# A two-layer graph convolution on one core: the last chunk sums interleaved with block 47's products, and block 48 placed in turned form

## The chip, the core and the metric

The kernel runs on one core of a Trainium2 chip. The metric is device time in microseconds (us). The kernel before took 2044.03 us in the median of three runs (2043.89 to 2047.14).

## The reference, cut to what matters

`x` is 6250 nodes by 512 features in fp32; `src` and `dst` are the 100,000 edges, sorted by `dst`. Two Chebyshev convolutions of order two follow each other:

```
h   = relu(layernorm(x))
deg = number of edges that leave a node;  dinv = deg > 0 ? 1 / sqrt(deg) : 0
conv(h, W0, W1, b) = h @ W0 + prop(h) @ W1 + b
prop(h)[n] = sum over edges e with dst[e] == n of  -dinv[src[e]] * dinv[n] * h[src[e]]
y   = leaky_relu(layernorm(conv(h, W1_0, W1_1, b1)) * gamma + beta)
out = x + conv(y, W2_0, W2_1, b2)
```

## The kernel before, in words

**Tiling.** Nodes are cut into 49 blocks of 128 rows (block 48 has 106). Edges are cut into 782 chunks of 128. Three chunks make a unit, four units a group, so there are 66 groups; group 0 holds one unit, group 65 the chunks 771 to 781 (its fourth unit has two chunks). Because `dst` is sorted, a unit's 384 edges fall into a window of 32 nodes, and a group's four windows stand below each other in the 128 rows of a PSUM tile.

**One group, in both layers.** GpSimd (POOL) gathers each chunk's 128 source rows from a table in DRAM by an indirect DMA (L444) into a ring of 55 places. VectorE (DVE) makes `sel`, a 0/1 matrix from edges to the window's 32 nodes (`choose`, L571); in layer 0 it scales `sel` by a column of the gathered rows (`scale`, L610). TensorE (PE) multiplies `sel` with the gathered rows, one matmul of 32 output rows and 512 columns for each chunk, summing a unit's three chunks into that unit's 32 rows (`sums`, L621). ScalarE (ACT) copies the 128 rows to SBUF (`agg`, L631).

**One block.** `place` (L651) moves the rows of the two or three groups that overlap the block to their place by 0/1 matrices `there` (made in `spots`, L639). ACT copies the result out, times `-dinv` (`an`, L704). Four PE transposes (L711) and a DVE copy (`aT`, L713) turn it, and `products` (L532) multiplies with the weights: four matmuls over slices `kc` of 128 features. The own-row product `h @ W0` is added in the same PSUM tile, or, for blocks 46 to 48 (`EARLY`), was computed earlier and is kept in `pre`. `finish` ends the block. In layer 0 that is the layer norm on DVE with steps on ACT (L671 to L688), then two writes by SyncE's queue (SP): the scaled rows to layer 1's table `tab[1]` (L685) and the rows themselves to `h_tab` (L690). In layer 1 it is an add (L660 for the last three blocks) and the write of the output (L665).

**Between the layers.** Layer 1's first 24 chunks are gathered before the last three blocks' rows exist (`gather_ahead`, L454): indices of those blocks are held to a row of zeros, and what is missing is added later by matmuls (L627) with counts that DVE and PE make from the edge list (`count_late`, L588 and L592). All later gathers of layer 1 (L444) wait until the last rows are in `tab[1]`.

**Order.** PE, POOL and SP run in the order in which the program is written; DVE and ACT are ordered by a scheduler, held back where the program says `issue_after`. In group step 64 (`g == NS - 2`) the code places block 47, sums units 0 and 1 of group 65 (six matmuls), turns block 47, places group 64's part of block 48 (`between`), multiplies block 47, and in the step of group 65 sums its units 2 and 3 (five matmuls). Then `turn` and `dense` do block 48: place group 65's part, copy out, transpose, copy, four products, `finish`. Only groups 64 and 65 overlap block 48.

Of the kernel before, what the change touches and what calls it, by code (L numbers as in the profile page):

```python
# [2 lines left out]

# [404 lines left out]
def usual_path(tc, have):  # L408
# [18 lines left out]
    with ExitStack() as es:  # L427
# [5 lines left out]
        own_h, own_x, agg, placed, started, pre, late, theres = {}, {}, {}, {}, {}, {}, {}, {}  # L433
        SHIFTED = D - D % P
        lidx = pool.tile([P, NC - SHIFTED], I32, name="lidx", bufs=1)

        def zr(layer, t):
            return places[:, (layer * NC + t) % R, :D]
# [91 lines left out]
        def products(u_ps, hT, w, r, start, stop):  # L530
            for kc in range(KD):
                nc.tensor.matmul(u_ps[:r], hT[:, kc, :r], w[:, kc, :], start=(start and kc == 0),  # L532
                                 stop=(stop and kc == KD - 1))

# [64 lines left out]
        def scale(sel, chunk, of=(0, NQ)):  # L599

            at = chunk[0][0]
            start = chunk[of[0]][0]
            end = chunk[min(of[1], len(chunk)) - 1][-1] + 1
            if end <= RAW:
                return
            each = sel.rearrange("p q s e -> p (q s) e")
            cut = sorted({start, end} | {t for t in range(start, end) if t % R == 0})
            for lo, hi in zip(cut, cut[1:]):
                v = each[:, lo - at : hi - at, :]
                last = nc.vector.tensor_tensor(  # L610
                    v, v, places[:, lo % R : lo % R + hi - lo, D : D + 1].to_broadcast([P, hi - lo, Q]), op=OP.mult)
            return last

        def sums(layer, g, sel, chunk, cnt=None, of=(0, NQ)):

            n = len(chunk)
            if of[0] == 0:
                summed[0] = psum.tile([P, D], F32, name="ps")
            ps = summed[0]
            for s, q in [(s, q) for s in range(STEP) for q in range(*of) if q < n and s < len(chunk[q])]:  # L620
                nc.tensor.matmul(ps[q * Q : (q + 1) * Q, :], sel[:, q, s, :], zr(layer, chunk[q][s]), start=(s == 0),  # L621
                                 stop=(s == len(chunk[q]) - 1 and (cnt is None or chunk[q][0] >= AHEAD_OF)))
# [6 lines left out]
            if of[1] >= n:  # L629
                agg[g] = pool.tile([P, D], F32, name="agg", bufs=3)  # L630
                nc.scalar.activation(agg[g][: n * Q], ps[: n * Q], AF.Copy)  # L631

# [10 lines left out]
        def place(i, some):  # L643

            r = rows[i]
            if i not in placed:
                placed[i] = psum.tile([P, D], F32, name="an_ps", bufs=1)
            there = theres.pop(i) if i in theres else spots(i, some)
            for t, g in zip(there, some):
                m = Q * (unit[g + 1] - unit[g])  # L650
                nc.tensor.matmul(placed[i][:r], t[:m, :r], agg[g][:m, :], start=(g == inside[i][0]),  # L651
                                 stop=(g == inside[i][-1]))

        def finish(layer, i, v):
            r = rows[i]
# [65 lines left out]
        def second(layer, i, aT):  # L721
            w1 = w_late[:, 0] if layer else w_sb[0]
            whole = i not in started
            u_ps = psum.tile([P, D], F32, name="u_ps") if whole else started.pop(i)
            products(u_ps, aT, w1, rows[i], whole, True)
            finish(layer, i, u_ps)
# [74 lines left out]
        for layer in range(2):  # L801
            if layer == 1:
                gathered = AHEAD_OF
                for i in range(AHEAD):
                    load(layer, i)
            i, chosen, left = 0, {}, []
            for g in range(NS):
                gather_to(layer, STEP * unit[g] + R)
                if layer == 0 and g == NS // 2:
                    for k, w in enumerate((W2_1, W2_0)):  # L810
                        nc.sync.dma_start(w_late[:, k], w.rearrange("(k p) d -> p k d", p=P))
                if layer == 0:
# [20 lines left out]
                of = (NQ // 2, NQ) if g == NS - 1 else (0, NQ)  # L833
                if layer == 0 and g < NS - 1:
                    with ExitStack() as order:
                        for ins in behind.values():
                            order.enter_context(tc.issue_after(ins.ins))
                        scaled = scale(sel, chunk)
                if g < NS - 1:
                    chosen[g + 1] = choose(g + 1)  # L840
                sums(layer, g, sel, chunk, count_late(sel, chunk) if layer == 1 else None, of)
                if layer == 0 and g == 1:
                    widen()
                if layer == 0 and g == NS - 16:
                    with tc.issue_after(scaled.ins):
                        shift(0, SHIFTED)
                        shift(SHIFTED, NC)
                if layer == 0:
                    look_up("hT_ps")
                    find("hT_ps")  # L850
                if g < NS - JOIN - 1 and inside[i].stop <= g + 1:
                    theres[i] = spots(i, inside[i])
                for k, (hT, an) in due:
                    if g < NS - JOIN:
                        left.append((k, first_half(layer, k, hT, an)))
                    else:
                        dense(layer, k, hT, an)
                if layer == 0:
                    look_up("hT_ps")
                    find("hT_ps")  # L860
                    if g >= NS // 2:
                        next(checking, None)
                for k, at in EARLY.items():
                    if g == at - 2:
                        load_early(layer, k)
                    if g == at:
                        early(layer, k)
                if g == NS - 2:
                    if layer == 0:
                        r = rows[NB - 1]  # L870
                        started[NB - 1] = psum.tile([P, D], F32, name="u_ps")
                        nc.tensor.matmul(started[NB - 1][:r], ident[:r, :r], pre[NB - 1][:r], start=True, stop=False)
                    assert i == NB - 2 and inside[i].stop < NS
                    hT, an = turn(layer, i)
                    if layer == 0:
                        with tc.issue_after(behind[1].ins), tc.issue_after(scaled.ins), tc.issue_after(behind_rows[0].ins):
                            scale(*chosen[g + 1], (0, NQ // 2))
                    sums(layer, NS - 1, *chosen[g + 1], None, (0, NQ // 2))

                    def between():  # L880
                        place(NB - 1, inside[NB - 1][:-1])
                        if layer == 0:
                            with tc.issue_after(behind[2].ins):
                                scale(*chosen[g + 1], (NQ // 2, NQ))
# [331 lines left out]
```

## Time and profile before

| what | us |
|---|---|
| median of three runs | 2044.03 |
| the profiled execution, its own time | 2042.93 |
| span of its instructions | 2041.0 |
| PE busy | 1678.5 |
| POOL busy | 1506.2 |
| DVE busy | 703.4 |
| ACT busy | 406.3 |

The span is the time from the first to the last instruction; 1.9 us of the profiled execution lie around it. Busy shares are averages over the whole span. Rows of a view are read as: start and length, engine, line, operation, output and inputs by the program's names, count, and in square brackets the idle time before the instruction and what ended it. `PEld` is the loading of weights into PE. One fp32 matmul leaves two records, a transpose one.

### The profile page before, as it was taken

Reading aid. Unit: us, or ns where it says so; the run is one execution under the profiler, and the core shown is the slowest. Engines: PE = TensorE matmul, PEld = TensorE weight load, DVE = VectorE, ACT = ScalarE, POOL = GpSimd, SP = SyncE. Lnnn points to the kernel's source line nnn. Section 1 sums busy time; section 2 is a strip of 40 time slices with the busy share of each in tenths; the row PEclk is TensorE's granted clock in tenths of the full one; section 3 lists DMA queues with packets and bytes.
Section 4 is the critical chain, followed back from the end, with each engine's and each line's share of the span. In section 5 each row is a group of like instructions: output and inputs, shape, how many; then the busy total and the mean of one; then the engine's idle time right before and its main releaser. Section 6 shows DMA issues by size and latency. Waiting matters only on the chain.

```text
span 2041.0 us, 19914 instructions
## 1 busy us (share of the span) xinstructions
PE 1678.5 (82%) x6838; PEld 662.6 (32%) x6838; DVE 703.4 (34%) x1483; ACT 406.3 (20%) x740; POOL 1506.2 (74%) x1578
## 2 busy tenths in 40 slices
PE   5579997778787767877889888888888888888887
PEld 4444432223333222333333332323332223333332
DVE  7975443232453333443462212122121212212221
ACT  7794221111211111221210101001010001011110
POOL 4677777777777777777777777777777777777774
PEclk9879998889988888988999988999998999999999
DMA  9998888888888888888887888887788888878875
GB/s 338 377 313 255 277 263 248 258 243 262 279 276 256 254 249 252 263 260 260 248 258 234 251 251 251 246 253 246 245 257 251 245 248 256 246 247 256 271 236 157
DMA packets 189414, 527.46 MB, mean 258 GB/s; under 512 B 34550, under 2 KB 36112, under 8 KB 189304
## 3 DMA queue, kind: packets, MB, share of 16 engines
q0 software_dynamic: 125120, 415.98, 68.0%
q1 hardware_dynamic: 64184, 110.12, 15.0%
q8 instruction: 56, 0.92, 0.2%
q14 instruction: 54, 0.44, 0.1%
HBM read 474.31 MB, written 51.66 MB: 258 GB/s over the span
## 4 chain that ended last, share of the span: by engine, by line
PE 42%; DMA 27%; POOL 14%; issue 11%; DVE 6%; ACT 1%; POOLq 0%; DVEq 0%; ACTq 0%; SPq 0%
DMA places<-tab,sidx 21%; PE u_ps L532 16%; POOL places L444 14%; PE ps L621 12%; PE an_ps L651 7%; DMA places<-tab,lidx 6%; PE hT_ps L711 1%; PE hT_ps L520 1%; DVE hi L340 1%; DVE lo L340 1%; PE hT_ps L492 1%; DVE st L671 0%; DVE sel L610 0%; PE both_ps L354 0%; DVE st L385 0%
## 5 line engine op out<-in xcount | busy, mean ns | idle before, releaser
L444 POOL DMA_INDIRECT places<-tab,sidx x1206 | 1145.0, 949 | 372.6 <-issue 266.2
L621 PE MATMUL ps<-places,sel 128*32 128x512 f32 x3128 | 531.6, 688 | 153.6 <-DMA places<-tab,sidx 84.9
L651 PE MATMUL an_ps<-agg,there 128*128 128x512 f32 (+1 forms) x580 | 281.6, 618 | 102.6 <-ACT agg L631 98.1
L444 POOL DMA_INDIRECT places<-tab,lidx x270 | 255.3, 945 | 82.3 <-issue 60.3
L621 PEld LDWEIGHTS ps<-places,sel 128*32 128x32 f32 x3128 | 106.3, 119 | 548.1 <-issue 196.5
L571 DVE TENSOR_TENSOR sel<-dlx,nodes_ps 128x384 f32<-128x384 f32 (+3 forms) x134 | 72.3, 541 | 424.8 <-PE ps L621 424.6
L631 ACT ACTIVATE agg<-ps 128x512 f32<-128x512 f32 (+1 forms) x132 | 78.4, 594 | 576.0 <-PE ps L621 553.6
L532 PE MATMUL u_ps<-w,hT 128*128 128x512 f32 (+1 forms) x392 | 178.7, 599 | 13.1 <-ACT hT L522 13.1
L651 PEld LDWEIGHTS an_ps<-agg,there 128*128 128x128 f32 (+1 forms) x580 | 108.9, 197 | 227.4 <-ACT agg L631 117.0
L532 PE MATMUL u_ps<-w,aT 128*128 128x512 f32 (+1 forms) x392 | 178.4, 598 | 2.5 <-DVE aT L713 2.5
L532 PE MATMUL u_ps<-places,hT 128*128 128x512 f32 (+1 forms) x392 | 176.9, 594 | 2.2 <-ACT hT L522 2.2
L532 PE MATMUL u_ps<-places,aT 128*128 128x512 f32 (+1 forms) x392 | 176.6, 593 | 1.5 <-DVE aT L713 1.5
L610 DVE TENSOR_TENSOR sel<-sel,places 128x384 f32<-128x384 f32 (+11 forms) x73 | 35.3, 485 | 375.1 <-DMA places<-tab,sidx 367.6
L662 DVE TENSOR_TENSOR u_ps<-u_ps,bias 128x512 f32<-128x512 f32 x46 | 32.2, 700 | 286.3 <-PE u_ps L532 286.3
L522 ACT ACTIVATE hT<-hT_ps 128x512 f32<-128x512 f32 (+1 forms) x98 | 58.2, 594 | 277.3 <-PE hT_ps L520 276.7
L639 DVE TENSOR_SCALAR there<-iota_r,node_of 128x128 f32<-128x128 f32 (+1 forms) x290 | 86.5, 301 | 60.9 <-PE an_ps L651 58.3
L704 ACT ACTIVATE an<-an_ps,ndinv 128x512 f32<-128x512 f32 (+1 forms) x98 | 67.1, 684 | 201.7 <-PE an_ps L651 201.4
L674 ACT ACTIVATE sd<-mv,eps 128x1 f32<-128x1 f32 (+1 forms) x49 | 14.4, 294 | 464.3 <-DVE mv L672 464.3
L236 POOL DMA_INDIRECT places<-in_x_dram,sidx x55 | 70.3, 1278 | 46.6 <-ACT junk L291 10.9
L532 PEld LDWEIGHTS u_ps<-w,aT 128*128 128x128 f32 (+1 forms) x392 | 72.5, 191 | 85.7 <-issue 79.4
L532 PEld LDWEIGHTS u_ps<-places,aT 128*128 128x128 f32 (+1 forms) x392 | 72.1, 190 | 83.1 <-issue 80.5
L532 PEld LDWEIGHTS u_ps<-w,hT 128*128 128x128 f32 (+1 forms) x392 | 71.3, 192 | 85.4 <-issue 71.7
(166 smaller groups left out, 1255.1 us busy)
## 6 DMA issues: line engine op xcount, KB each, us to landing
places<-tab,sidx POOLq DMA_INDIRECT x1206, 3.9
h_tab<-g SPq DMA_DIRECT2D x48, 256.0 KB, 5.8
xt<-in_x_dram SPq DMA_DIRECT2D x48, 256.0 KB, 5.1
out_dram<-t SPq DMA_DIRECT2D x48, 256.0 KB, 3.7
h<-tab SPq DMA_DIRECT2D x46, 256.0 KB, 5.0
tab<-t SPq DMA_DIRECT2D x46, 256.0 KB, 4.0
h<-h_tab SPq DMA_DIRECT2D x46, 256.0 KB, 4.5
tab<-places SPq DMA_DIRECT2D x22, 528.0 KB, 10.1
```

The source lines that it names most:

```text
L236: nc.gpsimd.indirect_dma_start(out=places[:, t, :D], out_offset=None, in_=x, in_offset=bass.IndirectOffsetOnAxis(ap=sidx[:, t : t + 1], ax ...
L340: nc.vector.tensor_tensor(t, s[:, g * 2 * GJ : (g + 1) * 2 * GJ].rearrange("p (j s) -> p j s", s=2)[:, :, None, :] .to_broadcast([EP, GJ, ...
L444: nc.gpsimd.indirect_dma_start(out=places[:, t % R, :] if own_scale else zr(layer, t), out_offset=None, in_=x if layer == 0 and t < RAW el ...
L522: nc.scalar.activation(hT[:, :, :r], ps[:, :, :r], AF.Copy)
L532: nc.tensor.matmul(u_ps[:r], hT[:, kc, :r], w[:, kc, :], start=(start and kc == 0), stop=(stop and kc == KD - 1))
L571: nc.vector.tensor_tensor(sel[:, q : q + k, :w, :], of, node[:, q : q + k, None, :].to_broadcast([P, k, w, Q]), op=OP.is_equal)
L610: last = nc.vector.tensor_tensor(v, v, places[:, lo % R : lo % R + hi - lo, D : D + 1].to_broadcast([P, hi - lo, Q]), op=OP.mult)
L621: nc.tensor.matmul(ps[q * Q : (q + 1) * Q, :], sel[:, q, s, :], zr(layer, chunk[q][s]), start=(s == 0), stop=(s == len(chunk[q]) - 1 and ( ...
L631: nc.scalar.activation(agg[g][: n * Q], ps[: n * Q], AF.Copy)
L639: behind[1] = nc.vector.tensor_scalar(t[:m, :r], iota_r[:m, :r], node_of[:m, g : g + 1], -(1.0 + i * P), op0=OP.subtract, op1=OP.is_equal)
L651: nc.tensor.matmul(placed[i][:r], t[:m, :r], agg[g][:m, :], start=(g == inside[i][0]), stop=(g == inside[i][-1]))
L704: nc.scalar.activation(an[:r], placed.pop(i)[:r], AF.Copy, scale=ndinv[:r, i : i + 1])
```

## The change

In both layers the sums of group 65 are cut differently: five of the six matmuls of units 0 and 1 stay ahead of block 47's transposes, and the sixth (chunk 776) joins the five of units 2 and 3 in a list `tail` whose order alternates between the units' rows: chunks 776, 777, 780, 778, 781, 779. Block 47's four products stand ahead of `tail` in layer 0. In layer 1 two stand ahead of it, one behind it, and one behind the last placing of block 48.

Block 48 is no longer placed as rows and then copied, transposed and copied. `place_end` takes 128 columns of `agg` as weights and a matrix `end_there` (nodes of the block, already times `-dinv`) as the moving operand, four matmuls of 106 columns for each group, and so writes the turned block; one DVE copy (`end_block`) brings it to SBUF. The two `end_there` matrices are made once, in steps 12 and 13 of layer 0, by four DVE instructions and one matmul. In layer 1 block 48's products, adds and writes are done in two halves of 256 columns.

Three `issue_after` edges also change: layer 1's `choose(1)` and the `count_late` of groups from 1 on are now held behind the last DVE instruction that makes rows of `tab[1]`.

```diff
+        def place_end(some):
+            r = rows[END]
+            if END not in placed:
+                placed[END] = psum.tile([P, KD, P], F32, name="an_ps", bufs=1)
+            for g in some:
+                m = Q * (unit[g + 1] - unit[g])
+                for kc in range(KD):
+                    nc.tensor.matmul(placed[END][:, kc, :r], agg[g][:m, kc * P : (kc + 1) * P], end_there[g][:m],
+                                     start=(g == inside[END][0] and kc == 0),
+                                     stop=(g == inside[END][-1] and kc == KD - 1))
+        def end_block(layer):
+            r = rows[END]
+            aT = pool.tile([P, KD, P], F32, name="hT", bufs=1)
+            nc.vector.tensor_copy(aT[:, :, :r], placed.pop(END)[:, :, :r])
+            return aT
+        def end_products(aT):
...
+            for lo in range(0, D, D // 2):
+                cols = slice(lo, lo + D // 2)
+                u_ps = psum.tile([P, D], F32, name="u_ps")[:, : D // 2]
+                products(u_ps, aT, w_late[:, 0, :, cols], r, True, True)
+                nc.vector.tensor_add(o[:r, cols], u_ps[:r], own[:r, cols])
+                for a, b in parts(r):
+                    nc.sync.dma_start(out[END * P + a : END * P + b, cols], o[a:b, cols])
...
-            for g in range(NS):
+            for g in range(NS - 1):
...
-                if g < NS - 1:
+                with ExitStack() as order:
+                    if layer == 1 and g == 0:
+                        order.enter_context(tc.issue_after(behind_rows[0].ins))
                     chosen[g + 1] = choose(g + 1)
-                sums(layer, g, sel, chunk, count_late(sel, chunk) if layer == 1 else None, of)
+                cnt = None
+                if layer == 1:
+                    with ExitStack() as order:
+                        if g > 0 and chunk[0][0] < AHEAD_OF:
+                            order.enter_context(tc.issue_after(behind_rows[0].ins))
+                        cnt = count_late(sel, chunk)
+                sums(layer, g, sel, chunk, cnt)
...
-                    sums(layer, NS - 1, *chosen[g + 1], None, (0, NQ // 2))
+                    head = [(s, q) for s in range(STEP) for q in range(NQ // 2)][:-1]
+                    one = [(STEP - 1, NQ // 2 - 1)] + [(s, NQ - 1) for s in range(len(at[NQ - 1]))]
+                    two = [(s, NQ // 2) for s in range(STEP)]
+                    tail = [k for both in zip_longest(one, two) for k in both if k]
+                    sums(layer, NS - 1, last, at, None, head, True, False)
                     def between():
-                        place(NB - 1, inside[NB - 1][:-1])
+                        place_end(inside[END][:-1])
...
-                    dense(layer, i, hT, an, between)
+                    aT = first_half(layer, i, hT, an, between)
+                    second(layer, i, aT, range(KD // 2) if layer else range(KD))
+                    sums(layer, NS - 1, last, at, None, tail, False, True)
+                    if layer:
+                        second(layer, i, aT, range(KD // 2, KD - 1))
+                    place_end(inside[END][-1:])
+                    end = end_block(layer)
+                    if layer:
+                        second(layer, i, aT, range(KD - 1, KD))
+                        end_products(end)
+                    else:
+                        second(layer, END, end)
                     i += 1
-            dense(layer, i, *turn(layer, i))
```

More of the change, by code (lines that the diff above doesn't have):

```diff
@@ L2 @@
 from contextlib import ExitStack
+from itertools import zip_longest
 import concourse.bass as bass
@@ L435, in usual_path @@
         lidx = pool.tile([P, NC - SHIFTED], I32, name="lidx", bufs=1)
+        END = NB - 1
+        end_there = {g: pool.tile([P, rows[END]], F32, name=f"end_there{g}", bufs=1) for g in inside[END]}
+        own_row, begun = {}, set()
         def zr(layer, t):
@@ L528, in load_x, with products @@
                 nc.sync.dma_start(own_x[i][lo:hi], x[i * P + lo : i * P + hi, :])
-        def products(u_ps, hT, w, r, start, stop):
-            for kc in range(KD):
+        def products(u_ps, hT, w, r, start, stop, some=range(KD)):
+            for kc in some:
                 nc.tensor.matmul(u_ps[:r], hT[:, kc, :r], w[:, kc, :], start=(start and kc == 0),
@@ L719, in first_half, with second @@
             return aT
-        def second(layer, i, aT):
+        def second(layer, i, aT, some=range(KD)):
             w1 = w_late[:, 0] if layer else w_sb[0]
[L723 to L726, printed above, removed]
+            if i not in started:
+                started[i] = psum.tile([P, D], F32, name="u_ps")
+                begun.add(i)
+            products(started[i], aT, w1, rows[i], i in begun and some[0] == 0, some[-1] == KD - 1, some)
+            if some[-1] == KD - 1:
+                begun.discard(i)
+                finish(layer, i, started.pop(i))
         def dense(layer, i, hT, an, between=None):
```

36 lines of the change are left out of this document (29 added, 7 removed).

## The prediction, as put on record before the run

> **What bounds the kernel now.** First the page's head, its costliest group and the waits of POOL in layer 1 (us in total, times, longest).
>
> ```profile
> span 2041.0 us, 19914 instructions
> ...
> PE 1678.5 (82%) x6838; PEld 662.6 (32%) x6838; DVE 703.4 (34%) x1483; ACT 406.3 (20%) x740; POOL 1506.2 (74%) x1578
> ...
> L444 POOL DMA_INDIRECT places<-tab,sidx x1206 | 1145.0, 949 | 372.6 <-issue 266.2
> ```
>
> ```profile
> POOL places L444 <- issue: 167.9, 551, 0.3
> ...
> POOL places L444 <- DMA tab<-pre: 3.4, 1, 3.4
> ```
>
> PE is busiest by share, but POOL sets the pace: a gather takes 0.95 us and the next starts 0.30 later, whatever the wait is put down to; no wait of layer 1 is longer, save one of 3.4. So 758 gathers of layer 1 (782 - 24) at 1.25 us make 948 us, from 1069.55 to the last one at 2017.33 (rows below). PE and DVE in the body of a layer have slack. Only two stretches end on something else: POOL's one stall between the layers, and the tail behind the last gather. The chain of work that ended last (start, length, what), from 2011 on:
>
> ```profile
> 2011.08 6.28 DMA places<-tab,lidx
> ...
> 2017.39 1.05 PE ps L621 x2
> 2018.44 0.59 PE hT_ps L711 x4
> 2019.03 0.86 PE an_ps L651 x2
> 2019.89 3.62 PE u_ps L532 x8
> 2023.51 2.71 PE ps L621 x10
> ...
> 2026.24 0.61 ACT agg L631
> ...
> 2026.89 1.12 PE an_ps L651 x2
> ...
> 2028.04 0.70 ACT an L704
> ...
> 2028.78 0.60 PE hT_ps L711 x4
> ...
> 2029.40 0.61 DVE aT L713
> ...
> 2030.05 3.70 PE u_ps L532 x8
> ...
> 2033.77 0.69 DVE t L660
> ```
>
> The reader sees PE held until 2017.39 by a chunk, then block 47 and block 48 one behind the other, each step waiting for the one above. From the last add's end (2034.46) to the span's end are 6.5 us of writing and closing, which move with it. The timeline around the last gathers, and their time to landing (min, median, max):
>
> ```profile
> 2014.48 2.76 PE L621 MATMUL ps<-places,sel 128*32 128x512 f32 x10
> ...
> 2016.08 0.95 POOL L444 DMA_INDIRECT places<-tab,lidx  x1 [0.30 <-issue]
> ...
> 2017.33 0.94 POOL L444 DMA_INDIRECT places<-tab,lidx  x1 [0.30 <-issue]
> ```
>
> ```profile
> DMA to landing us min/median/max: 3.4/3.9/7.7
> ```
>
> **The tail of layer 1, step by step.** (1) The sixth head sum (chunk 776) goes behind. The first five ended at 2014.48 + 2.76 = 2017.24, so the transposes start there and not at 2018.44: -1.2. Placing group 64 beside the copy of block 47's turned block is as long as before (step 4). (2) Two of block 47's four products go behind the sums: four of eight records of 3.62 us, -1.8. The sums then start at 2023.51 - 3.0 = 2020.5. Six matmuls instead of five still need three rounds, because the unit with chunks 777 to 779 alone needs three and the other units' run beside it: 2.7 as before. The last round starts about 1.75 in, at 2022.2, and needs the chunk issued at 2017.33, which at the median of 3.9 lands at 2021.2; the one before (2016.08) lands at 2020.0 and is needed at 2021.4. So nothing waits, with 1.0 us to spare. (3) Two products come back as fill: one beside `agg` (0.9 against 0.61 + 0.04), one beside the DVE copy (0.9 against 0.61 + 0.04): +0.25 each at most, I take +0.35 for both. (4) `place_end`: eight records with 128 columns of weights and 106 moving, in place of two with 512. No row shows them. The transposes of block 48 are nearest: four records of 128 columns of weights and 106 moving in 0.60. Eight cost 0.6 to 1.2; at the pace of the 512-column products (3.70 / 8 = 0.46 each) they would cost 3.7. I take 1.1, the nearest row's: no change against 1.12; the far end goes into the range as a rival. (5) `an` (0.70) and the transposes (0.60) go, with the gaps: the copy starts where `an` started, 2029.40 - 2028.04 = -1.36. What is then late is the same DVE copy, 0.61, now out of `an_ps`; on DVE the add of block 47 stands behind it, and needs the last product anyway. (6) Halved products cost the same columns; the first half's add and two of the four writes lie beside the second half's products. The last add falls from 0.69 to between 0.35 and 0.69; 424 columns against 512 in the copies (0.60 and 0.69) give 1 ns per column, so 0.43: -0.26. Its two writes are issued at the old distance; SP has only block 47's write and the first half's two before them, over 1.5 us earlier. The second half takes block 47's PSUM tile, free once that block's add has ended, beside the first half. Sum: -1.2 - 1.8 + 0.35 - 1.36 - 0.26 = **-4.3**.
>
> **Between the layers.** Rows of POOL and DVE from the timelines, and the same steps in the chain:
>
> ```profile
> 1060.76 1.67 POOL L454 DMA_INDIRECT places<-tab,eidx  x1 [0.30 <-issue]
> ...
> 1065.24 0.94 POOL L454 DMA_INDIRECT places<-tab,eidx  x1 [0.30 <-issue]
> 1069.55 1.36 POOL L444 DMA_INDIRECT places<-tab,sidx  x1 [3.37 <-DMA tab<-pre]
> 1071.22 1.10 POOL L444 DMA_INDIRECT places<-tab,sidx  x1 [0.30 <-PE hT_ps L592]
> ```
>
> ```profile
> 1058.89 0.69 DVE L688 TENSOR_TENSOR g<-u_ps,g 128x512 f32<-128x512 f32 x1 [0.66 <-ACT g L687]
> 1059.83 0.70 DVE L671 BATCH_NORM_STATS2 st<-u_ps 106x6 f32<-106x512 f32 x1 [0.25 <-PE u_ps L532]
> ...
> 1060.69 0.93 DVE L588 TENSOR_TENSOR t<-e_src,iota_r 128x768 bf16<-128x768 f32 x1
> ...
> 1062.26 0.54 DVE L588 TENSOR_TENSOR t<-e_src,iota_r 128x384 bf16<-128x384 f32 x1
> ...
> 1064.23 0.75 DVE L682 SCALAR_TENSOR_TENSOR pre<-u_ps,dinv,pre 106x512 f32<-106x512 f32 x1
> ```
>
> ```profile
> 1052.95 1.12 PE an_ps L651 x2
> ...
> 1054.09 0.70 ACT an L704
> ...
> 1055.45 0.61 DVE aT L713
> ```
>
> POOL has issued all it may at 1066.18 and waits for block 48's rows until 1069.55. Of that 0.30 is its usual gap, so at most 3.07 can be won, and all that is won moves layer 1's whole stream of gathers. Here all chunks have landed and all products stay ahead of the sums, so moving the sixth sum gives nothing: the sums take three rounds and end where they did. `an` and the transposes go as in the tail, 1055.45 - 1054.09: -1.36. On DVE, block 48's stats start then at 1058.5. In the changed program's order the two L588 (0.93 and 0.54, of which the gaps show about 1.3 on the path) go behind L682, and block 47's `g` (0.69) comes in behind the stats: -0.5, between -0.2 and -0.7. One new wait: DVE's copy of the turned block stands ahead of block 47's L676 to L682 and waits for the placing until about 1054.1. Behind it wait ACT and block 47's write; but that block's `g` stood at 1058.89, after its rows, which so have some 5 us over block 48's (1064.98).
>
> Against this: the 0/1 matrices of L588 now run while POOL issues gathers again. At 1060.76 a gather took 1.67 instead of 0.95 beside an L588, and 1069.55 and 1071.22 show 1.36 and 1.10. I take +0.4 for later L588, between 0 and 1.4 (two more at 0.7). [...] Sum between the layers: -1.36 - 0.5 + 0.4 = **-1.5**, between 0 and -3.07.
>
> **What costs nothing.** The four new DVE instructions and one matmul of steps 12 and 13 replace four of the same size in the tails, 0.30 each (L639); they fall before a stretch where PE waits for gathers (columns: us, PE, PEld, DVE, ACT, POOL busy, clock, DMA):
>
> ```profile
> L639 DVE TENSOR_SCALAR there<-iota_r,node_of 128x128 f32<-128x128 f32 (+1 forms) x290 | 86.5, 301 | 60.9 <-PE an_ps L651 58.3
> ```
>
> ```profile
> 310.00:330.00 20.00, 11.53 (x44) 3.78 (x42) 0.63 (x2) 0.00 (x0) 15.13 (x17) 0.86 0.81 246
> ```
>
> Without that cover they cost 1.5 us at most. Layer 1's first counts and `sel` come about a microsecond later; PE has 39 us (31 gathers) before POOL needs a place of layer 1 again.
>
> **Sum.** -4.3 - 1.5 = -5.8 us. The profiled execution took 2042.93, so 2037.1 in its own terms; it lies 1.1 under the median of 2044.03, so **2038.3** as a median.
>
> **Rivals.**
>
> *The transition gives nothing* (0.10). Block 48's rows land later by the spread of a DMA, or L588 eats the rest. Then only the tail counts: 2039.7. For it: the 1.67; against it: 1.36 us of removed work stand straight on the path.
>
> *The last landing takes over* (0.07). At the largest landing of 7.7 us the chunk arrives at 2025.0 and the last round starts 2.8 later: 2041.1. It decides from a landing above 4.9; the median says no.
>
> *The changed order does not overlap* (0.05), that is, the sums are not taken as they land. If the alternating rows ran one record after another, 12 x 0.45 = 5.4 instead of 2.7 at each end: 2043.7. Against it: ten records of two units took 2.71, half of ten in a row.
>
> *The clock* (0.05). Rows of stretches of 3.4 us, and of products at half clock:
>
> ```profile
> 1027.66:1031.07 3.41, 0.86 (x6) 0.56 (x6) 3.41 (x8) 1.97 (x3) 2.50 (x4) 1.00 0.79 222
> 1031.07:1034.48 3.41, 3.41 (x5) 1.35 (x6) 0.94 (x3) 0.00 (x0) 2.51 (x3) 0.50 0.86 239
> 2027.75:2031.17 3.42, 1.95 (x8) 0.99 (x8) 0.60 (x1) 0.69 (x1) 0.00 (x0) 1.00 0.01 2
> ```
>
> ```profile
> 1030.93 5.40 PE u_ps L532 x8
> ```
>
> A stretch with 0.86 us of PE work is followed by one at clock 0.50, and eight records took 5.40 instead of 3.70; after 1.95 us of work (2027.75) they took 3.70. If the halving met the last products, +1.7 for a stretch, +3.4 for two, so 2040.0 to 2041.7. [...]
>
> *Slower: the small records do not stream* (0.06). If each of `place_end`'s records costs what a 512-column one costs, 0.46, a placing takes 3.7 instead of 1.1: +2.6, on the path in four places (groups 64 and 65, both layers): +10.4 - 5.8, so 2048.7. It turns the sign from about 0.3 us a record (5.8 over 32 records, on 0.14). For it: weights change at every record; against it: the transposes do too, at 0.15.
>
> **How the numbers follow.** The forecast itself has 0.67. About 0.2% (4.1 us) is what a measurement of this kernel can tell from no change, so faster means below 2039.9: forecast and the first rival, 0.77. Within 0.2%: landing, overlap and clock, 0.17. Slower: 0.06. The range takes the whole 3.07 of the stall at its lower end (2036.7) and 0.9 of the fill and add terms, 2035.8; above it reaches past the late landing and most of the clock case, 2041.5.
>
> **What would show it.** Right: transposes of block 47 right behind five sums; no `an` and no transposes for block 48; its DVE copy right behind `place_end`'s eight records of some 1.1 us; POOL's stall at 1.2 to 2.0 instead of 3.37; 12.8 us from the last gather's start to the last add's end, 17.1 before (2034.46 - 2017.33). Wrong: `place_end` above 2 us, sums waiting for chunk 781, a half clock in the last products, or a longer stall.

## The result, and the profile after

The changed kernel took 2039.68 us in the median of 16 runs (2035.40 to 2042.12), the kernel before 2044.07 in 16 runs beside it (2039.21 to 2048.08). By the medians that is 4.4 us less. The ratio of the two, from all their runs, is 0.9976, 95% interval [0.9968, 0.9985]: 4.9 us less, between 3.1 and 6.5. The forecast was 5.8 less. Where a run below has both, microseconds are given by the ratio. The profiled execution of the changed kernel took 2041.34 us, 1.7 above its median; it is the third longest of the 16, which matters below. In its code the gathers stand at L448 and L458, the sums at L627, `products` at L536, `place_end` at L680, its copy at L688, the half adds at L700, the counts at L592, block rows at L732 and their write at L735, `g` at L737 and L738, `an` at L754, transposes at L761, `aT` at L763.

The page's head and the costliest group:

```profile
span 2039.4 us, 19969 instructions
...
PE 1675.8 (82%) x6864; PEld 669.4 (33%) x6864; DVE 702.2 (34%) x1484; ACT 404.8 (20%) x738; POOL 1517.1 (74%) x1578
...
L448 POOL DMA_INDIRECT places<-tab,sidx x1206 | 1147.3, 951 | 370.8 <-issue 272.2
```

Nothing has changed in the body of a layer: a gather still takes 0.95 us and PE and DVE do the same work. The end of the chain of work that ended last (start, length, what), which answers to the chain shown of before:

```profile
2017.46 2.69 PE ps L627 x10
2020.15 0.59 PE hT_ps L761 x4
2020.74 0.87 PE an_ps L680 x8
2021.61 1.89 PE u_ps L536 x4
2023.51 2.70 PE ps L627 x12
2026.20 1.06 PE u_ps L536 x2
2027.26 0.87 PE an_ps L680 x8
2028.13 4.48 PE u_ps L536 x18
...
2032.63 0.42 DVE t L700
```

The reader sees the changed tail as it was drawn up: transposes right behind five head sums, two products (four records), six sums in three rounds, one product as fill beside `agg`, `place_end`, one product as fill beside the copy, block 48 in halves. ACT and the transposes of block 48 are gone from the chain. From the start of the first head sum to the last add's end are 2033.05 - 2017.46 = 15.59 us. Before it was 2034.46 - 2014.48 = 19.98: **4.4 less, and 4.3 was the sum of the steps.** But the last gather stands here at

```profile
2016.58 0.95 POOL L448 DMA_INDIRECT places<-tab,lidx  x1 [0.30 <-issue]
```

so from the last gather to the last add are 16.47 us, where 12.8 was forecast (17.1 before): PE comes late to the tail, its head sums begin 0.9 *after* the last gather's start and not 2.9 before it.

Between the layers, POOL's and then DVE's and ACT's rows from the timelines:

```profile
1066.69 1.19 POOL L448 DMA_INDIRECT places<-tab,sidx  x1 [2.17 <-DMA tab<-pre]
1068.18 1.96 POOL L448 DMA_INDIRECT places<-tab,sidx  x1 [0.31 <-issue]
1070.45 1.09 POOL L448 DMA_INDIRECT places<-tab,sidx  x1 [0.30 <-issue]
```

```profile
1060.63 0.75 DVE L732 SCALAR_TENSOR_TENSOR pre<-u_ps,dinv,pre 106x512 f32<-106x512 f32 x1 [0.76 <-ACT pre L731]
...
1067.44 1.42 DVE L592 TENSOR_TENSOR t<-e_src,iota_r 128x384 bf16<-128x384 f32 x2
```

```profile
1063.74 0.60 ACT L737 ACTIVATE g<-u_ps 106x512 f32<-106x512 f32 x1 [3.15 <-DMA h_tab<-g]
```

The stall, POOL's wait between the layers, is 2.17 instead of 3.37 us (1.2 to 2.0 was forecast). Block 48's rows were ready at 1061.38 (L732), and the gather that needs them went at 1066.69, 5.3 later; before it was 1064.98 and 1069.55, 4.6. So in this pair of profiles 0.7 of the earlier rows went into a longer way of the write. That the change lengthens it is not shown. The write and the gather of run e1 below, whose layer 0 ends as before, are 5.7 us apart:

```profile
1065.19 0.72 SPq L735 DMA_DIRECT2D tab<-pre  x2
```

```profile
1070.91 1.00 POOL L448 DMA_INDIRECT places<-tab,sidx  x1 [3.86 <-DMA h<-h_tab]
```

(There the trace puts the end of the wait down to another transfer.) In the changed kernel the gather at 1068.18 took 1.96 us beside the counts of L592. And there is a wait that no step had: block 48's `g` shares one buffer with block 47's, and ACT waits 3.15 us until that has been written to `h_tab`; the counts behind it on DVE so move further into the resumed gathers.

### The profile page after: what moved, and what is told of

Read it like the earlier page. It is cut to its first block, busy times and chain, and to the rows that moved or that the text cites. A ratio compares the mean times of both kernels' runs of the same rounds, so it can differ in the third digit from the quotient of the medians.

```text
span 2039.4 us, 19969 instructions
## 1 busy us (share of the span) xinstructions
PE 1675.8 (82%) x6864; PEld 669.4 (33%) x6864; DVE 702.2 (34%) x1484; ACT 404.8 (20%) x738; POOL 1517.1 (74%) x1578
## 4 chain that ended last, share of the span: by engine, by line
PE 45%; DMA 23%; POOL 13%; issue 11%; DVE 6%; ACT 1%; DVEq 0%; POOLq 0%; ACTq 0%; SPq 0%
PE u_ps L536 18%; DMA places<-tab,sidx 16%; PE ps L627 14%; POOL places L448 13%; PE an_ps L657 8%; DMA places<-tab,lidx 6%; PE hT_ps L761 2%; PE hT_ps L524 2%; DVE hi L341 1%; DVE lo L341 1%; PE hT_ps L496 1%; DVE sel L614 1%; DVE st L721 0%; DMA places<-in_x_dram 0%; DVE u_ps L718 0%
## 5 line engine op out<-in xcount | busy, mean ns | idle before, releaser
L448 POOL DMA_INDIRECT places<-tab,sidx x1206 | 1147.3, 951 | 370.8 <-issue 272.2
L627 PE MATMUL ps<-places,sel 128*32 128x512 f32 x3128 | 521.2, 683 | 154.9 <-DMA places<-tab,sidx 84.1
L448 POOL DMA_INDIRECT places<-tab,lidx x270 | 255.7, 947 | 82.3 <-issue 63.4
L627 PEld LDWEIGHTS ps<-places,sel 128*32 128x32 f32 x3128 | 104.5, 119 | 542.5 <-issue 200.8
L536 PE MATMUL u_ps<-w,hT 128*128 128x512 f32 (+1 forms) x400 | 182.3, 599 | 14.8 <-ACT hT L526 14.1
L536 PE MATMUL u_ps<-places,hT 128*128 128x512 f32 (+2 forms) x408 | 183.4, 593 | 2.2 <-ACT hT L526 2.2
L536 PE MATMUL u_ps<-w,aT 128*128 128x512 f32 x384 | 174.6, 598 | 1.8 <-DVE aT L763 1.8
L536 PE MATMUL u_ps<-places,aT 128*128 128x512 f32 x384 | 173.3, 593 | 0.8 <-DVE aT L763 0.8
L712 DVE TENSOR_TENSOR u_ps<-u_ps,bias 128x512 f32<-128x512 f32 x46 | 32.2, 700 | 289.1 <-PE u_ps L536 289.1
L237 POOL DMA_INDIRECT places<-in_x_dram,sidx x55 | 79.0, 1437 | 36.6 <-issue 8.8
L754 ACT ACTIVATE an<-an_ps,ndinv 128x512 f32<-128x512 f32 x96 | 65.8, 685 | 203.4 <-PE an_ps L657 203.3
L536 PEld LDWEIGHTS u_ps<-w,hT 128*128 128x128 f32 (+1 forms) x400 | 72.6, 192 | 88.8 <-issue 73.2
L536 PEld LDWEIGHTS u_ps<-places,hT 128*128 128x128 f32 (+1 forms) x408 | 74.7, 193 | 76.5 <-issue 72.3
L536 PEld LDWEIGHTS u_ps<-w,aT 128*128 128x128 f32 x384 | 71.5, 192 | 82.1 <-issue 78.1
```

The lines of the kernel that those rows point to most:

```text
L237: nc.gpsimd.indirect_dma_start(out=places[:, t, :D], out_offset=None, in_=x, in_offset=bass.IndirectOffsetOnAxis(ap=sidx[:, t : t + 1], ax ...
L448: nc.gpsimd.indirect_dma_start(out=places[:, t % R, :] if own_scale else zr(layer, t), out_offset=None, in_=x if layer == 0 and t < RAW el ...
L754: nc.scalar.activation(an[:r], placed.pop(i)[:r], AF.Copy, scale=ndinv[:r, i : i + 1])
```

## The experiments

Theory after the result: the tail of layer 1 is worth its 4.3 us, and the transition (the change between the layers) less than 1.5 because the write and the counts take back what the shorter steps give. Rivals: the gain comes from the transition and the tail's is lost to PE; or the turned placing does it all and the order of sums and products nothing. Edits are shown against the changed kernel; ratios are to the kernel before, measured beside each run.

**One layer at a time (e1, e2).**

```diff
+                    if layer == 1:        # e1;  e2: layer == 0
                         head = ...        # the changed end of the layer
+                    else:
+                        ...               # sums, place and dense as before the change
```

> The change in layer 1 alone; layer 0 ends as before. Theory (the two ends add up, the tail carries most): 3.3 to 4.3 us under the kernel before, about 2040.3 as a median; in the profile POOL's stall between the layers stays near 3.4 us, and from the first sums of group 65 to the last add are 15.7 us instead of 20.0 (or 18.9 where before would not have waited for chunk 776). Rival (the gain comes from the transition): within 1 us of the kernel before.

> The change in layer 0 alone; layer 1 ends as before. Theory: POOL's stall falls from 3.4 to about 2.2 us, but the gathers after it are held up about 0.9 us longer by the count matrices and the rows' writes take 0.7 longer to land, so only some 0.7 us of the time goes: about 2043.3. Rival (the stall won is won in full, or all of the 4.4 is won here): 2041 or lower.

Layer 1 alone: 2036.4 us against 2040.16, ratio 0.9979 [0.9970, 0.9988], 4.3 us less (3.8 by the medians). Layer 0 alone: 2038.86, ratio 0.9997 [0.9988, 1.0006], 0.6 less (1.3 by the medians) and not told apart from nothing. The two add up to the whole within their intervals: most of the gain is the tail's.

How much of it is the tail's own? In e2, whose layer 1 ends as before, the sixth head sum found its chunk landed:

```profile
2015.22 2.70 PE ps L627 x12
...
2033.25 0.69 DVE t L710
```

The old tail took 18.72 us there from the first head sum to the last add's end, and not 19.98. Against this the new one (15.59 in e1, 15.60 in e10) is worth 3.1. So the 1.2 us of step 1 are won only where the sixth sum has to wait for chunk 776, as in the profile of the kernel before. Counted from the last gather's start the old tail took 17.1 (before) and 16.8 (e2), the new one 13.4 (e1 and e10). The time of e1, between 2.4 and 6.1 us less, holds 3.1 as well as 4.3.

**The turned placing without the new order (e3).** Six head sums ahead of the transposes, all four products ahead of the five other sums, in both layers; block 48 turned and halved as in the change.

```diff
-                    head = [(s, q) for s in range(STEP) for q in range(NQ // 2)][:-1]
+                    head = [(s, q) for s in range(STEP) for q in range(NQ // 2)]
...
-                    tail = [k for both in zip_longest(one, two) for k in both if k]
+                    tail = [(s, q) for s in range(STEP) for q in range(NQ // 2, NQ) if s < len(at[q])]
-                    second(layer, i, aT, range(KD // 2) if layer else range(KD))
+                    second(layer, i, aT)
...
```

> Block 48 placed in turned form in both layers and layer 1's halves kept, but sums and products in the order of before (six sums, block 47's four products, five sums). Theory: the tail gains only the copy, the transposes and the half add, 1.36 + 0.26 = 1.6 us, the transition 0.7: about 2.3 us under before, 2041.7, and 18.0 us or more from the first sums of group 65 to the last add. Rival (the placing is all of the gain, since PE has to do the same sums and products anyway): 4.4 us under before, as the whole change.

2038.0 us, ratio 0.9990 [0.9981, 0.9999], 2.0 less. By the time, the turned placing and the halves give somewhat under half, and the order of sums and products the rest. Steps 5 and 6 had 1.6 in layer 1 for the first, steps 1 to 3 had 2.65 for the second. But in the tail of e3's profile something else is at work. Its chain of work, then its stretches (us, PE, PEld, DVE, ACT, POOL busy, clock, DMA), then the same 16 products in the changed kernel:

```profile
2009.92 2.70 PE ps L627 x12
...
2022.97 5.40 PE u_ps L536 x16
...
2028.39 0.42 DVE t L700
```

```profile
2020.13:2023.55 3.42, 1.97 (x12) 1.46 (x12) 0.60 (x1) 0.60 (x1) 0.00 (x0) 1.00 0.01 2
2023.55:2026.96 3.41, 3.41 (x10) 2.37 (x9) 0.42 (x1) 0.00 (x0) 0.00 (x0) 0.50 0.03 7
```

```profile
2028.89 3.70 PE L536 MATMUL u_ps<-places,hT 128*106 128x256 f32 x16
```

From the first head sum to the last add's end e3 took 18.89 us, no less than e2's old tail. Its last products met a half clock and took 5.40 instead of 3.70: the clock rival of the prediction, with its 1.7 us, came true in this kernel. Without it the tail would be 17.2, which is 1.5 under e2's 18.72, as steps 5 and 6 had it. PE had waited for `agg` and for the copy of the turned block just ahead. In the whole change the products put there as fill leave no such wait, and in its two profiles the last products took 3.70. So part of what the time gives to the order may be the clock; how many of e3's timed runs met it is not known.

**The counts beside the gathers (e4).** The index of the rows gathered ahead is moved from SBUF into spare columns of a PSUM tile, so that each count reads one SBUF operand instead of two. That the place of an operand decides how long a gather beside a count takes was not shown by any run ahead of this one.

```diff
-    e_src = const.tile([P, AHEAD_OF, LATE], F32, name="e_src")
...
+    e_src = nodes_ps[:, D - P - AHEAD_OF * LATE : D - P].rearrange("p (c b) -> p c b", b=LATE)
```

> The whole change, with the counts' index columns in PSUM instead of SBUF, so that those DVE instructions have one input in SBUF. [...]

2031.84 us, ratio 0.9958 [0.9945, 0.9972]: 8.6 less than before, about 4 less than the changed kernel. The groups of gathers from 1058 to 1092 us (count, busy, mean ns of one), first of the changed kernel, then of e4:

```profile
L448 POOL DMA_INDIRECT places<-tab,sidx x19 | 20.2, 1062 | 7.7 <-issue 3.4 <-DMA tab<-pre 2.2 <-DMA places<-tab,sidx 0.9
```

```profile
L448 POOL DMA_INDIRECT places<-tab,sidx x22 | 20.8, 946 | 6.7 <-issue 4.3 <-DMA places<-tab,sidx 1.8 <-PE ps L627 0.6
```

In e4 no gather is longer beside a count: 16 counts ran from 1061.3 to 1085.9 us, and each gather there took 0.94 or 0.95 us; 946 ns against 1062 is 19 x 0.116 = 2.2 us. So beside counts with one input in PSUM the gathers kept their usual time, and beside counts with both inputs in SBUF some took up to 1.96. The stall, however, went too, and the operand does not explain that. With the index in that tile the scheduler also moved the first count out from among block 46's steps. So e4 had changed two things. The rows that show the second, PE and DVE of the changed kernel, then PE of e4:

```profile
1029.27 5.39 PE L536 MATMUL u_ps<-w,aT 128*128 128x512 f32 x8 [1.78 <-DVE aT L763]
```

```profile
1027.02 0.94 DVE L592 TENSOR_TENSOR t<-e_src,iota_r 128x768 bf16<-128x768 f32 x1
1027.89 0.73 DVE L732 SCALAR_TENSOR_TENSOR t<-u_ps,dinv,t 128x512 f32<-128x512 f32 x1
1028.55 0.67 DVE L763 COPY aT<-hT_ps 128x512 f32<-128x512 f32 x1
```

```profile
1028.57 3.70 PE L536 MATMUL u_ps<-w,aT 128*128 128x512 f32 x8 [0.78 <-DVE aT L763]
```

A count that layer 1 needs 30 us later stood ahead of block 46's copy, PE waited 1.78 instead of 0.78 us, and its eight records then took 5.39 instead of 3.70. This was in the kernel before as well (the 5.40 of the prediction's clock rival).

**Order or operand (e5, e9, with the changed kernel again as e10).** The index stays in SBUF, and the first count is held behind block 48's rows.

```diff
-                        if g > 0 and chunk[0][0] < AHEAD_OF:
+                        if chunk[0][0] < AHEAD_OF:
```

> The whole change, and group 0's count matrices of layer 1 held behind block 48's rows like the others; the index stays in SBUF. It tells apart what e4 did by its order from what it did by its operand. Theory (order and clock): the count instruction of 0.94 us that stands on VectorE ahead of block 46's aT copy is gone from there, TensorE waits 0.8 instead of 1.78 us before block 46's products, no half-clock window follows, those products take about 3.6 instead of 5.4 us, and GpSimd's stall between the layers falls from 2.17 to under 0.5 us; the counts still lengthen gathers, by 2 to 4 us in all, so the time comes out between the changed kernel's and 2 us under it, and some 2 to 4 us above e4. Rival (operand alone): the stall stays near 2.2 us and the time is the changed kernel's or up to 2 us above it.

In that measurement data moved more slowly: the kernel before took 2481.74 us and e5 2473.28, ratio 0.9964 [0.9943, 0.9985]. The rate, and POOL's waits (us in total, times, longest), in e5's profile:

```profile
HBM read 474.31 MB, written 51.66 MB: 212 GB/s over the span
```

```profile
POOL places L448 <- remote: 214.7, 89, 4.8
...
POOL places L448 <- DMA tab<-pre: 22.2, 1, 22.2
```

In the first measurement the same bytes moved at 258 GB/s. With a stall of 22 us, a microsecond of DVE's order is out of sight. So it ran again:

> The kernel of e5 once more: in e5's call the kernel before itself took 2481.7 us, its gathers' data moved at 213 instead of 260 GB/s, and the stall between the layers was 22 us, so that call could not tell the theories apart. On a chip where the kernel before takes some 2040 us they stand as they did. Theory (order and clock): TensorE waits 0.8 instead of 1.78 us ahead of block 46's products, these take 3.6 instead of 5.4 us, GpSimd's stall falls from 2.17 to under 0.5 us, and the time is the changed kernel's or up to 2 us less. Rival (operand alone): the stall stays near 2.2 us and the time is the changed kernel's or up to 2 us more.

> The changed kernel itself, beside e9 on the same chip, so that the two can be compared. Theory: 4 to 5 us under the kernel before as in the first measurement; with TensorE not behind in layer 1's last blocks, 12.8 to 13.4 us from the last gather's start to the last add's end, as in e1 and e4 (13.4 and 13.0), not 16.5 as in the first profile; the half-clock window near 1030 us and the stall of about 2.2 us are there again. Rival (the half-clock window near 1995 us and TensorE's lag belong to the change): 16 us again.

e9 took 2036.9 us, ratio 0.9969 [0.9959, 0.9979]; the changed kernel beside it 2038.34, ratio 0.9978 [0.9966, 0.9989]; before, 2042.81. PE's rows of e9, then its stretches of 3.4 us there (us, PE, PEld, DVE, ACT, POOL busy, clock, DMA), then the same stretches of the changed kernel's first profile:

```profile
1029.14 3.70 PE L536 MATMUL u_ps<-w,aT 128*128 128x512 f32 x8 [0.78 <-DVE aT L763]
```

```profile
1026.34:1029.75 3.41, 1.85 (x8) 0.79 (x7) 2.98 (x8) 1.46 (x3) 2.50 (x4) 1.00 0.78 212
1029.75:1033.17 3.42, 3.42 (x12) 1.23 (x14) 1.51 (x4) 0.60 (x1) 2.58 (x3) 1.00 0.85 240
```

```profile
1025.90:1029.31 3.41, 0.85 (x6) 0.46 (x5) 3.41 (x8) 1.97 (x3) 2.50 (x4) 1.00 0.77 208
1029.31:1032.73 3.42, 3.42 (x4) 1.46 (x5) 1.04 (x3) 0.00 (x0) 2.81 (x3) 0.50 0.90 243
```

With the count gone, PE works 1.85 of 3.41 us, the next stretch keeps the full clock, and the products take 3.70; with the count, 0.85 us of work, and the next stretch runs at 0.50. POOL's stall was 0.30 in e9, its usual gap: the whole 3.07 us of the transition can be had. But the median is only 1.4 us under the changed kernel's (1.8 by the ratios, whose intervals overlap). Two things take from the 3 us: the stall of the changed kernel was not 2.17 every time (0.51 in e10's profile, where two gathers ahead of it took 1.36 and 1.31 us and so used up 0.8), and the counts now all meet gathers. The gathers of e9 from 1058 to 1092 us:

```profile
L448 POOL DMA_INDIRECT places<-tab,sidx x19 | 19.4, 1024 | 5.8 <-issue 4.3 <-PE ps L627 0.6 <-DMA places<-tab,eidx 0.3
L458 POOL DMA_INDIRECT places<-tab,eidx x7 | 7.8, 1109 | 2.1 <-issue 1.5 <-PE hT_ps L596 0.3 <-DMA places<-tab,eidx 0.3
```

19 x 0.078 + 7 x 0.163 = 2.6 us over e4's 946 ns each. By the ratios e9 is 2.2 us above e4, by the gathers 2.6. So e4's gain over the changed kernel, about 4 us though the two were not timed side by side, is made of both: some 2.2 by the operand and 1.8 by the order, each with an uncertainty near its own size; the rows, not the times, part them. The rival (operand alone) has the stall against it.

**The clock by itself, and two more (e6, e7, e8, e11, e12).** e6 and e11 leave the count where it stood and give PE something to do in the wait:

```diff
                 begun.add(i)
+                if layer == 0 and i == END - 2:
+                    for k in range(2):
+                        nc.tensor.matmul(started[i], ident, gam, start=True, stop=True)
```

e7 is e4 with block 48's `g` in an `xt` buffer, so that ACT has no write to wait for; e8 and e12 are the kernel before with e4's line.

> The whole change, and two more matrix products (ident by gam, 4 records, about 1.8 us) in layer 0 into block 46's empty product tile, where TensorE waits 1.78 us for the aT copy; the products behind them overwrite the tile. Theory (clock): the window of 3.41 us before block 46's products is then busy enough, the next is not halved, the eight records take 3.6 instead of 5.4 us, and the stall of GpSimd between the layers falls by 1 to 1.7 us; the time is 1 to 1.7 us under the changed kernel's. Rival (the half window costs nothing in the median run, or the fillers push the products back as much as they gain): within 0.5 us of the changed kernel.

> As e4 (the whole change with the index in PSUM), and block 48's g in a buffer of another name, so that ScalarE does not wait for block 47's h_tab write. Theory: that wait delayed only the last block's h_tab write and the counts behind it, which no longer lengthen gathers, so within 0.7 us of e4 (about 8.5 us under the kernel before). Rival (the late counts hold up the first sums of layer 1): 2 us or more under e4.

> The kernel before, with nothing but the index of the rows gathered ahead moved into spare columns of the PSUM tile. Theory: that gain has nothing to do with the change: the order on VectorE before block 46's aT copy and the counts beside the gathers are the same in both, so 3 to 4 us under the kernel before, and the change on top of it (e4) is worth 4 to 5 us as without it. Rival: the index helps only where the change has taken the rest of the stall, and this kernel is within 1 us of the kernel before.

> The kernel of e6 again, on a chip like the first (e6's was the one with the slow transfers). It parts the two halves of e9's gain: the count instruction stays ahead of block 46's aT copy on VectorE, so TensorE's products still start 1.8 us after the transposes, but two extra products (1.8 us) fill that time. Theory (clock): no half-clock window follows near 1030 us, block 46's eight records take 3.7 us as in e9 and not 5.2 to 5.4, the write of block 48's rows is issued 1.5 us sooner after the first gather ahead than in the changed kernel's profiles (26.9 and 25.8 us), and the stall is under 0.7 us; the time is up to 1.5 us less than the changed kernel's, 5 to 6 us under the kernel before. Rival (only the count's place on VectorE counted): half-clock window and 5.2 us as in e10.

> The kernel of e8 again, on a chip like the first: the kernel before, with the index of the rows gathered ahead in spare columns of the PSUM tile and so, as in e4, with the counts behind block 48's rows. Theory: the gain is there without the change: TensorE's wait ahead of block 46's products, the half-clock window, the stall of 3.4 us and the lengthened gathers beside the counts (1.4 us) all shrink, so 3 to 4.5 us under the kernel before. Rival: it was worth that only with the change; within 1 us of the kernel before.

All of these met the slow transfers (before: 2481.74 and 2454.66 us). Ratios: e6 0.9964 [0.9944, 0.9983], e7 0.9967 [0.9944, 0.9989], e8 0.9993 [0.9971, 1.0015], e11 0.9992 [0.9959, 1.0025], e12 1.0015 [0.9981, 1.0050]. As times they settle nothing for the faster transfers. What the filler does on PE can still be read, from e6's rows:

```profile
1252.66 1.88 PE L778 MATMUL u_ps<-gam,ident 128*128 128x512 f32 x4
1254.60 3.70 PE L536 MATMUL u_ps<-w,aT 128*128 128x512 f32 x8
```

The count is still ahead of the copy on DVE, the products start where they would have, and with the wait filled they take 3.70 us; e11's took 3.70 as well. In all six profiles with the count ahead and the wait left empty (before, the changed kernel's two, e1, e2, e3) they took 5.16 to 5.40. So the half clock goes with PE's idle time and not with the count, save that no profile without the filler was taken under the slow transfers; what that alone is worth in the median is not shown. Nor is it settled whether the index in PSUM helps the kernel before by as much: e8 and e12 gave nothing, where a stall of over 20 us can hide all of it. e7 was not compared with e4 side by side.

**PE's late arrival in the tail.** The profiles of the runs above show it. The last gather, and the last add, of e10, then of e1:

```profile
2015.98 0.94 POOL L448 DMA_INDIRECT places<-tab,lidx  x1 [0.30 <-issue]
```

```profile
2028.93 0.42 DVE t L700
```

```profile
2020.40 0.95 POOL L448 DMA_INDIRECT places<-tab,lidx  x1 [0.30 <-issue]
```

```profile
2033.40 0.42 DVE t L700
```

13.4 us in both, and 13.0 in e4, where 12.8 was forecast. In the first profile it was 16.5 and in e9's 16.2. The stretches that part them, of the changed kernel's first profile and of e10:

```profile
1991.88:1995.29 3.41, 1.46 (x7) 0.31 (x5) 0.00 (x0) 0.07 (x1) 2.51 (x3) 1.00 0.94 345
1995.29:1998.70 3.41, 3.41 (x8) 1.86 (x8) 0.69 (x1) 0.53 (x1) 2.79 (x3) 0.50 0.77 217
```

```profile
1989.83:1993.24 3.41, 2.25 (x14) 0.44 (x12) 0.00 (x0) 0.04 (x1) 2.73 (x3) 1.00 0.91 320
1993.24:1996.65 3.41, 3.41 (x12) 1.74 (x12) 0.69 (x1) 0.56 (x1) 2.57 (x3) 1.00 0.72 220
```

It is one kernel in both. Chunks land late between 1990 and 1994, and PE idles. In e10 it waited 0.32 and 0.84 us; in the first profile it waited 1.95 in one piece:

```profile
1994.14 1.05 PE L627 MATMUL ps<-places,sel 128*32 128x512 f32 x2 [1.95 <-DMA places<-tab,lidx]
```

This left 1.46 us of work in the stretch, and the next ran at half clock. From there to the end PE has only two waits of 0.78 us in which it could catch up. e9, the other late one, had 1.59 us of work in a stretch there and a half clock behind it. The stretches do not fall at the same place of the program in these two executions: one begins 21.3 us before the last gather in the first profile and 22.7 in e10's, 1.4 apart, which is less than one stretch. The first profile caught the worse case. That this is why its own time lies above the median is not shown: the profiled execution of e1 took 2042.05 us, 5.7 above its median, with PE in time. How many of the timed runs had it is not known.

## Why the prediction was right, and where it was off

- **Steps 1 to 6, the tail: -4.3.** 4.4 from head sum to last add in the first profile, 4.3 by e1, 13.0 to 13.4 instead of 12.8 from the last gather wherever PE arrives in time. Right against the profile from which it was read, in part by luck: the 1.2 of step 1 hang on a chunk that took 6.28 us to land in that one execution. Against e2's old tail the new one is worth 3.1.
- **Steps 5 and 6: -1.6.** 1.5 by e3's rows, once the half clock that it met is taken off.
- **Step 3, fill: +0.35.** `place_end` began 0.4 after `agg` had ended, behind the first fill product, and the second cost nothing (the copy ended at 2028.84, the next products began at 2028.89); right.
- **Step 4, `place_end`: 1.1 us.** 0.87 in the chain where another record follows. The rival of small records at 0.46 each is out by a factor of four.
- **Step 6, half add: 0.43.** 0.42.
- **Between the layers: -1.5.** e2 gave -0.6, and its interval, -2.4 to +1.2, holds -1.5; the interval of the whole, -3.1 to -6.5, holds -5.8. So this is the likeliest place of the 0.9 to 1.4 us by which the forecast went too far, but it is not shown. The removed steps went as said (`an`, transposes and DVE's order: the tail sums to L732 took 15.48 and now 13.55, -1.93 against -1.86). In the first profile 0.9 was left of it: the stall is 1.2 shorter and the gathers ahead of it 0.5, but those behind it are held up 2.2 us (five of them) and not 1.4 (four), which is 0.8 more where +0.4 was taken. That profile, however, was the least favourable of four. From the first gather ahead to the first gather behind the stall took 33.8 us before and 33.7 in e1, which has the old transition, and 32.2, 32.1, 31.0 and 31.0 with the new one (first profile, e2, e3, e10). With what the gathers behind the stall were held up, 35.2 and 34.1 stand against 34.3, 33.1, 32.9 and 32.2. The spread among executions of one kernel is as large as the term.
- **"1.36 us of removed work stand straight on the path."** True, and yet the stall is no fixed length: in the four profiles with the changed transition and the count in its old place (first profile, e2, e3, e10) it was 2.17, 2.17, 0.79 and 0.51. In the first profile what ended it was the landing of one write (2.17 us, `<-DMA tab<-pre`), not the row before it alone; and it also shrinks, without any gain, when the gathers ahead of it are held up (0.8 us in e10).
- **The rival of the clock** was given only a cost, in the last products. The changed kernel's last products did not meet it; e3's did, behind a stretch with 1.97 us of work. In the changed end of layer 0 it was not met either: the stretch from 1049.81 in the first profile has 2.03 us of work, and the next ran at 1.00. It decided elsewhere too, at 1995 us in the first profile, and at 1030 both kernels' products had been taking 1.7 us longer all along. The row that showed the half clock was itself the place of a gain.
- **The rivals of the last landing and of the order** did not come: six sums took 2.70.

The best version that ran is e4, 8.6 us under the kernel before, 0.9958 [0.9945, 0.9972].

## What to carry to other kernels

Work that is taken out of a dependent tail can come back whole in the time, when no wait takes its place; work taken out ahead of a stall that ends with a transfer comes back only as far as the transfer lands earlier and what runs behind the stall is not held up in turn. Before a wait is counted as won, see whether another execution has it at all. When a TensorE product takes 1.5 times its usual time (here 5.39 us instead of 3.70, behind 3.41 us with 0.85 us of work), look at the 3.4 us before it: here an idle TensorE just ahead of the critical work cost twice, 1.0 us more of waiting and 1.7 in the products, and the cause was an instruction that nobody needed yet, standing in a queue ahead of it. One profile is one execution: before a difference from the forecast is explained, see whether a second profile of the same kernel has it.

## What the runs showed of the hardware

- Beside DVE's counts with both inputs in SBUF, GpSimd's indirect gathers took up to 1.96 us instead of 0.95 (changed kernel), and beside the same counts with one input in PSUM none took longer (e4: 946 ns each over 22 gathers). What links the two is not shown.
- In the changed kernel's first profile, cut from 1.93 us on into 596 stretches of 3.413 us, the granted clock was 1.00 in 491 and 0.50 in 105, and nothing between. After a stretch of 3.41 us with little PE work the next ran at half clock: 0.85, 1.30 and 1.46 us of work (changed kernel), 1.59 (e9). But the busy time alone does not decide. 1.76 us (before, from 1065.20) and 1.97 (e3, from 2020.13) were also followed by a half clock, while 1.39 (changed kernel, from 735.79), 1.85 (e9) and 1.95 (before, from 2027.75) were not.
- The kernel before took 2040 to 2044 us in the medians of three measurements, and 2482 and 2455 in two others, with 212 GB/s (e5) instead of 258, a stall between the layers of over 20 us, and (in e5's profile) some 200 us of POOL's waits on releases that the trace cannot name. What slows the transfers there is open. The measurement with e9 (2042.81) and that with e11 (2454.66) carry the same chip number, so it need not belong to the chip.
